# Four stacked graph-attention layers: the last stages of the last pairs turn and spread through TensorE instead of through transfers

## The chip, the core and the metric

The kernel runs on one core of one Trainium2 chip. A core has five engines with a queue of instructions each: TensorE (PE in the profile; its weight loads are PEld), VectorE (DVE), ScalarE (ACT), GpSimd (POOL) and SyncE (SP), which here only issues transfers (DMA). Each queue is worked off in its order, and engines wait for each other by semaphores. The metric is the device time in microseconds (us), a median over runs.

## The reference

Each of 128 graphs has 128 nodes with 512 features, and a 128 x 128 adjacency matrix. Four layers follow one another, each `x = layernorm(x + attention(x, adj))`. In short:

```
for layer in (L0, L1, L2, L3):            # x: (128 graphs, 128 nodes, 512 features)
    e    = leaky_relu(s_src[:, :, None] + s_dst[:, None, :], 0.2)   # per head
    attn = softmax(where(mask(adj), e, -inf))
    x    = layernorm(x + f(attn @ h(x)))
# L0: 1 head, h(x) = x
# L1: two nested layers: 4 heads of 256 (x @ W1, elu), then 1 head of 512 (h @ W2); the mask is turned
# L2: 8 heads of 64 (x @ W)
# L3: 1 head, f = elu
```

All is in 32-bit floats. An attention needs one score of every node along the rows (a column, a bias of ScalarE) and the other score along the free axis, the same in all 128 partitions (the column "spread"). Its weights come out as rows by columns and must be turned before they can be multiplied by TensorE; so must `x` before a projection.

## The kernel before

Graphs are worked on in 64 pairs (two graphs, `g`). `pair(n)` writes the work of one pair as a list of operations: `first` (layer L0), a projection by w1 in Strassen's seven products (`strassen`, the matmuls of line 711), `second` (the four-headed half of L1), a projection by w2, `third` (its one-headed half), a projection by w3, `fourth` (layers L2 and L3, and the output, line 976). Nothing is executed yet. `plan` gives each operation a due time: the length of the longest chain of work behind it, stretched by `STRETCH`; pair n starts 44.5 us (`PACE`) after pair n - 1. `lay_out` then walks through all operations with a model of costs and chooses for every engine the next operation that can start, the earliest due one first. This gives a fixed order for each queue; at run time the queues keep it, whatever the waits are. It also places the tiles in SBUF (one large `arena`) and in the eight PSUM banks. Several pairs are in work at any time; after the last pair has entered, the queues run empty, and what is left is the last pairs' later stages.

Three helpers matter here.

- `spread(cols)` brings columns of scores along the free axis. VectorE turns a broadcast of them in blocks of 32 (line 598), a transfer writes the turned rows to DRAM (line 602, tile `row`), and one or two transfers read them back into all 128 partitions (line 607, tile `db`).
- `turned(srcs, n)` turns n tiles of 128 x 128. VectorE turns the 32 x 32 blocks (line 620, into `zb`), a transfer writes them to DRAM (line 624, `scr`), and another reads them back with the blocks exchanged (line 633, or 628 for `second`; into `pt`).
- `attend(db, h0, nh, src, mask)` is the softmax of nh heads: the leaky relu on ScalarE, out of `db` into a PSUM bank (line 647); the mask and the row's extreme on VectorE (line 654, which at the same time writes its rows in the block order that `turned` expects); the exponential with its sum on ScalarE (line 663); the reciprocal (line 671); where asked for, a multiplication by it on GpSimd (line 673).

`norm` is the layer norm: statistics on VectorE (lines 682 and 686), the root on ScalarE (691, 692), the offset on GpSimd (697, 698), the scaling on ScalarE (702). `mixed` is the matmul attention times values (line 780), `resid` adds the residual on VectorE (786); `sums` prepares Strassen's left sides on GpSimd (734).

`third` calls `spread` with 2 columns, `turned` with 2 tiles, and `turned` with 8 tiles (x2, for w3). `fourth` calls `spread` with 16 columns, `turned` with 8 tiles for each graph, the matmuls of the eight heads (line 934, scaled by lines 940, and added to x2 by GpSimd on line 945), a norm, four small GpSimd operations (956 to 959) for the scores of L3, `spread` with 2 columns, `turned` with 2 tiles, `mixed`, then elu (ACT 968, DVE 970), the residual (POOL 974), a norm, and the output. So a pair issues 6 such transfers in `third` and 11 in `fourth`. In `first`, `x1` is normed in place, turned, and b2 is added to it on GpSimd into a second tile `xb` (line 846).

Of the kernel before, what the change touches and what calls it, by code (L numbers as in the profile page):

```python
# [13 lines left out]
AF = mybir.ActivationFunctionType  # L14
ALU = mybir.AluOpType
# [9 lines left out]


STRETCH, PACE, AHEAD = 1.28, 44.5, 80.0
HOP = {"PE": 0.0, "DVE": 0.0, "ACT": 0.5, "POOL": 1.0, "SP": 2.0}
SEED, SPREAD = 1, 0.0
BANKS, PRODUCTS = 8, 2  # L30
SEES = {"PE": 0.06, "DVE": 0.06, "ACT": 0.06, "POOL": 0.06, "SP": 0.0}
TAIL = {"PE": 0.165, "DVE": 0.09, "ACT": 0.1, "POOL": 0.05, "SP": 0.0}
# [69 lines left out]
def plan(ops):  # L102

    before = needs(ops)
    after = [[] for _ in ops]
    for k, need in enumerate(before):
        for q in need:
            after[q].append(k)
    left = [0.0] * len(ops)
    for k in reversed(range(len(ops))):  # L110
        left[k] = ops[k].least() + HOP[ops[k].engine] + max((left[q] for q in after[k]), default=0.0)
    rng = random.Random(SEED)
    return [STRETCH * (max(left) - left[k]) + SPREAD * rng.random() for k in range(len(ops))]


def lay_out(ops):
# [142 lines left out]
def tile_gat_stack(  # L259
# [316 lines left out]
    def bank():  # L576
        return Buf("ps", [P, 512])
# [9 lines left out]

    def spread(cols, split=1):

        n = sum(k for _, k in cols)  # L590
        sT, row = Buf(f"sT{n}", [P, n, 32]), Buf(f"row{n}", [n, P])
        a = 0
        for (b, col), k in cols:
            def turn(col=col, a=a, k=k):
                c, o = col(), sT.ap[:, a : a + k, :]
                if len(c.shape) > 2:
                    o = o.rearrange("p (a b) c -> p a b c", a=c.shape[1])
                nc.vector.transpose(o, c.unsqueeze(len(c.shape)).to_broadcast([*c.shape, 32]))

            op("DVE", 0.06 + 0.04 * k, turn, [b], joins=[sT])  # L600
            a += k
        op("SP", 0.6, lambda: nc.sync.dma_start(
            out=row.ap.rearrange("h (b c) -> b h c", b=P // 32), in_=sT.ap[0:P:32]
        ), [sT], [row], dma=0.03 + 0.01 * n, desc=4 * n)
        dbs, m = [Buf(f"db{n // split}", [P, n // split, P]) for _ in range(split)], n // split
        for i, db in enumerate(dbs):
            op("SP", 0.5, lambda i=i, db=db: nc.sync.dma_start(
                out=db.ap.rearrange("p h j -> p (h j)"),
                in_=row.ap[i * m : (i + 1) * m].rearrange("h j -> (h j)").partition_broadcast(P),
            ), [row], [db], dma=0.06 + 0.1825 * m, desc=P)  # L610
        return dbs

    def turned(srcs, n, moving=False):


        zb, scr = Buf(f"zb{n}", [P, 4, n, 32]), Buf(f"scr{n}", [P, n * P])
        o = Buf(f"pt{n}", [P, 4, n, 32] if moving else [P, n, P])
        m = n // len(srcs)
        for a, (b, src) in enumerate(srcs):
            op("DVE", 0.075 + 0.134 * m, lambda a=a, src=src: nc.vector.transpose(  # L620
                zb.ap[:, :, a * m : (a + 1) * m, :].rearrange("p b h c -> p h b c"),
                src().rearrange("p h (b c) -> p h b c", c=32),
            ), [b], joins=[zb])
        op("SP", 0.5, lambda: nc.sync.dma_start(
            out=scr.ap, in_=zb.ap.rearrange("p b h c -> p (b h c)")
        ), [zb], [scr], dma=0.05 + 0.19 * n, desc=P)
        if moving:
            op("SP", 0.58, lambda: nc.sync.dma_start(
                out=o.ap.rearrange("p q h c -> p q (h c)"),
                in_=scr.ap.rearrange("p f -> (p f)").rearrange("(q p e) -> p q e", q=4, p=P),  # L630
            ), [scr], [o], dma=0.215 * n, desc=4 * P)
        else:
            op("SP", 0.7, lambda: nc.sync.dma_start(
                out=o.ap.rearrange("p h (q c) -> p h q c", q=4),
                in_=scr.ap.rearrange("p f -> (p f)").rearrange("(q p h c) -> p h q c", q=4, p=P, h=n),
            ), [scr], [o], dma=0.415 * n, desc=4 * P * n)
        return o

    def attend(db, h0, nh, src, mask, scaled=False):

        z = bank()
        zz, nm, rs, ri = (Buf(f"{t}{nh}", s) for t, s in (
            ("zz", [P, nh, P]), ("nm", [P, nh]), ("rs", [P, nh]), ("ri", [P, nh])))

        def prelu():
            for h in range(nh):
                nc.scalar.activation(  # L647
                    z.ap[:, h * P : (h + 1) * P], db.ap[:, h0 + h, :], AF.Prelu, bias=src[1]()[:, h : h + 1], alpha=SLOPE
                )


        def masked():
            for h in range(nh):
                nc.vector.tensor_tensor_reduce(  # L654
                    out=zz.ap[:, h, :].rearrange("p (b a) -> p a b", b=4),
                    in0=z.ap[:, h * P : (h + 1) * P].rearrange("p (a b) -> p a b", b=4),
# [8 lines left out]
                    accum_out=rs.ap[:, h : h + 1],  # L665
                )

        op("ACT", [0.4] * nh, prelu, [db, src[0]], [z])
        op("DVE", [0.24] * nh, masked, [z, mask[0]], [zz, nm])
        op("ACT", [0.387] * nh, exp, [zz, nm], [zz, rs])  # L670
        op("DVE", 0.06, lambda: nc.vector.reciprocal(ri.ap, rs.ap), [rs], [ri])  # L671
# [133 lines left out]
    def first(n):  # L805
# [11 lines left out]
        for s, wv, init in ((1, w0d, 0.0), (0, w0s, b0t)):  # L817
# [4 lines left out]
                    accum_out=sc0.ap[:, s, g : g + 1],  # L822
                ), [x0], [jk], joins=[sc0], uses=[*w0b, b0b], port=True)
            if s:
                db, = spread([(part(sc0, 1), 2)])
        mask(m2, at, ALU.is_le)
        pm = bank()

# [5 lines left out]
        op("DVE", 0.335, lambda: nc.vector.tensor_mul(  # L834
            m1.ap, pm.ap[:, : 2 * P].rearrange("p (g j) -> p g j", g=2), over(noneye)
        ), [pm], [m1])
        zz, ri = attend(db, 0, 2, part(sc0, 0), (m0, lambda h: m0.ap[:, h, :]))
        pt = turned([part(zz)], 2)
        x1 = [Buf("x1", [P, F]) for _ in G]
        for g in G:  # L840
            resid(x1[g], mixed(pt, g, part(x0, g)), ri, g, part(x0, g))
        norm([part(b) for b in x1])
        xT = turned([(b, lambda b=b: wide_rows(b.ap)) for b in x1], 8)
        xb = [Buf("xb", [P, F]) for _ in G]
        for g in G:
            op("POOL", 1.24, lambda g=g: nc.gpsimd.tensor_add(xb[g].ap, x1[g].ap, b2t), [x1[g]], [xb[g]], uses=[b2b])
        return dict(xT=xT, xb=xb, m1=m1)

    def second(st, xl):

        m1 = st["m1"]
        scores = lambda g, s: part(xl[g], every, slice(2 * FH + 2 * s, 2 * FH + 2 * s + 2))
        db, = spread([(scores(g, 0), 4) for g in G])
        zz = []
        for g in G:
            def col(g=g):
                return Four(xl[g].ap)

            zz.append(attend(db, 4 * g, 4, (xl[g], col), (m1, lambda h, g=g: m1.ap[:, g, :]), scaled=True)[0])
        pt = turned([part(z) for z in zz], 8, moving=True)  # L860
        hT = [[Buf("hT", [P, 4, P]) for _ in range(2)] for _ in G]
        for g in G:
# [32 lines left out]
    def third(st, xl2):  # L895

        m1, xb = st["m1"], st["xb"]
        sc2 = small("sc2", 2)
        db, = spread([(part(xl2, every, 0, F // 2), 2)])
        op("DVE", 0.07, lambda: nc.vector.tensor_add(  # L900
            sc2.ap, xl2.ap[:, :, 1, F // 2], shift2.ap
        ), [xl2], [sc2], uses=[shift2], port=True)
        zz, ri = attend(db, 0, 2, part(sc2), (m1, lambda h: m1.ap[:, h, :]))
        pt = turned([part(zz)], 2)
        x2 = [Buf("x2", [P, F]) for _ in G]
        for g in G:
            resid(x2[g], mixed(pt, g, part(xl2, g, every, slice(0, F // 2)), True), ri, g, part(xb[g]))
        norm([part(b) for b in x2])
        st["x2"] = x2
        st["xT2"] = turned([(b, lambda b=b: wide_rows(b.ap)) for b in x2], 8)  # L910

    def fourth(n, st, xl3):

        x2 = st["x2"]
        at, m2, m3 = edges(n, xl3), Buf("m2", [P, 2, P]), Buf("m3", [P, 2, P])
        mask(m2, at, ALU.is_le)
        dbs = spread([(part(xl3[g], every, slice(SH, SH + 4)), H2) for g in G], 2)
        z3 = [Buf("z3", [P, H2, CH]) for _ in G]
        x3 = [Buf("x3", [P, F]) for _ in G]
        sc4, sz = small("sc4", 2, 2), small("sz", 2, 2)  # L920
# [1 line left out]
            op("POOL", 0.2, lambda g=g: nc.gpsimd.tensor_copy(sc4.ap[:, g, :], xl3[g].ap[:, :, C3 - 1]), [xl3[g]], joins=[sc4])  # L922
        for g in G:
            both = [attend(
                dbs[g], 4 * q, 4, part(xl3[g], q, slice(SH + 4, SH + 8)), (m2, lambda h, g=g: m2.ap[:, g, :])
            ) for q in range(2)]
            pt = turned([part(zz) for zz, _ in both], 8)
            for q in range(2):
# [30 lines left out]
            nc.gpsimd.tensor_add(sc4.ap, sc4.ap, sw.ap)  # L959

        op("POOL", 0.9, normed, [sc4, sz, rd, md], [sc4, sw], uses=[swf])
        db, = spread([(part(sc4, every, 1), 2)])
        zz, ri = attend(db, 0, 2, part(sc4, every, 0), (m3, lambda h: m3.ap[:, h, :]), scaled=True)
        pt = turned([part(zz)], 2)
        y = Buf("y", [P, 2, F])
        pas = [mixed(pt, g, part(x3[g])) for g in G]
# [10 lines left out]
            out=out[2 * n : 2 * n + 2].rearrange("g p f -> p g f"), in_=y.ap  # L977
        ), [y], [], dma=1.58, desc=2 * P)

    def pair(n):  # L980
        st = first(n)
        xT = st["xT"]
        xl = [Buf("xl1", [P, 2, N1]) for _ in G]
# [2 lines left out]
        for j in range(2):  # L986
            cols = slice(j * C1, (j + 1) * C1)
            strassen(left, s, w1s, 2, C1, cols, lambda g, h, cols=cols: xl[g].ap[:, h, cols], xl, w1_ready)
        hT = second(st, xl)
        xl2 = Buf("xl2", [P, 2, 2, C2])  # L990
        left = [[part(t) for t in both] for both in hT]
        strassen(left, sums(left, [P, 4, P]), w2s, 4, C2, slice(0, C2), lambda g, h: xl2.ap[:, g, h, :], [xl2, xl2], w2_ready)
        third(st, xl2)
        xT2 = st["xT2"]
        xl3 = [Buf("xl3", [P, 2, C3]) for _ in G]
        left = [[part(xT2, slice(4 * g + 2 * a, 4 * g + 2 * a + 2)) for a in range(2)] for g in G]
        strassen(left, sums(left, [P, 2, P]), w3s, 2, C3, slice(0, C3), lambda g, h: xl3[g].ap[:, h, :], xl3, wh_ready)
        fourth(n, st, xl3)

    pairs = B // 2  # L1000
    offsets = None
    for n in range(pairs):
        begin = len(ops)
        pair(n)
        if offsets is None:
            own = ops[begin:]
            offsets = plan(own)
        for o, t in zip(ops[begin:], offsets):
            o.due = n * PACE + t

    names = {}

# [50 lines left out]
```

## Time and profile before

| what | value |
|---|---|
| median of 3 runs (lowest, highest) | 3069.99 us (3069.07, 3072.15) |
| profiled execution: its time, its span | 3071.79 us, 3070.0 us |
| PE, DVE, ACT, POOL busy | 94 %, 84 %, 80 %, 72 % of the span |
| DMA engines, mean over the span | 605.64 MB moved, 197 GB/s |
| mean granted TensorE clock | 0.975 of full speed |
| the outputs of the last six pairs (58 to 63) are issued at | 2915.96, 2953.41, 2990.66, 3022.76, 3048.01 and 3066.22 us |

The page lists busy time by engine, the span in forty slices (a digit is a busy share in tenths), the DMA queues, the chain of work that ended last, and the costliest groups of instructions. In a timeline row stand the start, the duration, the engine, the line, the operation with output and input tiles, a count where equal ones are merged, and in brackets how long the engine had been idle and what ended that. In a row of a table by stretches stand, for each engine, busy us and the number of instructions; then the granted clock, the share of the DMA engines, and GB/s. A 32-bit matmul is two MATMUL instructions in the trace, a turning on TensorE one.

### The profile page before, as it was taken

The numbers are of one execution on the slowest core, as the hardware profiler recorded it, in microseconds if no ns is written. First come the engines' busy times: TensorE is split into PE (matmuls) and PEld (weight loads), VectorE is DVE, ScalarE is ACT, GpSimd is POOL, SyncE is SP. The second block draws the span as 40 slices with busy tenths as digits, with TensorE's granted clock in tenths as the row PEclk, the third lists the DMA queues.
The fourth block names the chain that finished last, engine by engine and source line by source line (L and its number), as shares of the span: only waits on it lengthen the run. The fifth ranks groups of instructions, "written<-read, shape, count | busy, mean of one in ns | idle before, by whom it ended". The sixth has DMA issues, their size and how long they took to land.

```text
span 3070.0 us, 56562 instructions
## 1 busy us (share of the span) xinstructions
PE 2876.5 (94%) x14054; PEld 2347.5 (76%) x14054; DVE 2585.8 (84%) x9269; ACT 2445.8 (80%) x8229; POOL 2215.9 (72%) x2859
## 2 busy tenths in 40 slices
PE   5799999999999999999999999999999999999863
PEld 3588778888888888888888888887888888888742
DVE  4768888898888889889888988898898889888763
ACT  2367888888888888888888888888888888888763
POOL 4766677777777777777777777777777777877632
PEclk8799999999999999999999999999999999999986
DMA  3369899999899999999999999989989999988774
GB/s 109 95 159 202 194 207 219 201 208 220 199 213 211 219 200 211 213 212 206 210 221 196 213 209 216 204 208 221 197 215 207 219 202 208 223 196 207 179 149 93
DMA packets 1500859, 605.64 MB, mean 197 GB/s; under 512 B 1285962, under 2 KB 1400650, under 8 KB 1500532
## 3 DMA queue, kind: packets, MB, share of 16 engines
q1 hardware_dynamic: 1499164, 598.87, 86.2%
q8 instruction: 114, 1.87, 0.3%
q14 instruction: 213, 1.74, 0.2%
q0 software_dynamic: 576, 2.10, 0.2%
q10 hardware_dynamic: 792, 1.06, 0.1%
HBM read 374.43 MB, written 227.48 MB: 196 GB/s over the span
## 4 chain that ended last, share of the span: by engine, by line
PE 44%; ACT 22%; DVE 15%; issue 4%; DMA 1%; POOL 1%; DVEq 0%; ACTq 0%; SPq 0%; POOLq 0%
PE ps L711 31%; ACT ps L647 10%; PE ps L934 6%; PE ps L780 5%; DVE arena L620 4%; DVE st L682 3%; ACT arena L702 3%; DVE arena L756 3%; ACT arena L968 2%; ACT arena L663 2%; DVE arena L654 2%; ACT arena L879 2%; ACT arena L719 2%; DVE arena L786 1%; DMA arena<-scr 1%
## 5 line engine op out<-in xcount | busy, mean ns | idle before, releaser
L734 POOL TENSOR_TENSOR arena<-arena 128x256 f32<-128x256 f32 (+1 forms) x768 | 682.1, 903 | 238.2 <-DVE arena L880 80.1
L711 PE MATMUL ps<-w1s,arena 128*128 128x258 f32 x3584 | 810.5, 383 | 36.1 <-DMA arena<-scr 35.7
L711 PEld LDWEIGHTS ps<-w1s,arena 128*128 128x128 f32 x3584 | 683.6, 191 | 192.8 <-issue 55.3
L711 PE MATMUL ps<-w2s,arena 128*128 128x257 f32 x3584 | 822.4, 380 | 4.9 <-DVE arena L880 3.0
L711 PEld LDWEIGHTS ps<-w2s,arena 128*128 128x128 f32 x3584 | 678.8, 190 | 139.1 <-issue 30.1
L663 ACT ACTIVATE arena<-arena,nm 128x128 f32<-128x128 f32 x1920 | 742.0, 396 | 30.9 <-DVE nm L654 28.9
L654 DVE CUSTOM_DVE_ANT_0 arena<-ps,arena 128x128 f32<-128x128 f32 x1920 | 531.1, 381 | 189.6 <-ACT ps L647 186.4
L647 ACT ACTIVATE ps<-arena 128x128 f32<-128x128 f32 x1536 | 564.1, 371 | 89.7 <-DMA arena<-row 52.1
L620 DVE STREAM_TRANSPOSE arena<-arena 128x512 f32<-128x512 f32 (+1 forms) x832 | 527.9, 635 | 83.0 <-ACT arena L702 52.0
L711 PE MATMUL ps<-w3s,arena 128*128 128x273 f32 x1792 | 475.9, 400 | 67.2 <-ACT arena L719 42.4
L719 ACT COPY arena<-ps 128x258 f32<-128x258 f32 (+2 forms) x1024 | 346.7, 377 | 197.9 <-PE ps L711 182.4
L711 PEld LDWEIGHTS ps<-w3s,arena 128*128 128x128 f32 x1792 | 329.6, 192 | 140.9 <-issue 50.0
L702 ACT ACTIVATE arena<-arena,mr,rd 128x512 f32<-128x512 f32 x512 | 401.3, 811 | 24.8 <-POOL mr L698 24.8
L780 PE MATMUL ps<-arena 128*128 128x512 f32 x768 | 375.0, 610 | 25.6 <-DMA arena<-scr 16.3
L663 ACT ACTIVATION_READ_ACCUMULATOR arena<-arena,nm 128x1 f32 x1920 | 373.9, 195 | 0.0
L756 DVE TENSOR_TENSOR arena<-ps,arena 128x258 f32<-128x258 f32 (+2 forms) x768 | 311.3, 412 | 68.8 <-PE ps L711 47.8
L682 DVE BATCH_NORM_STATS2 st<-arena 128x6 f32<-128x512 f32 x512 | 343.1, 680 | 13.6 <-POOL arena L945 6.9
L791 POOL TENSOR_SCALAR arena<-arena 128x256 f32<-128x256 int32 x256 | 299.0, 1168 | 32.3 <-DMA arena<-in_adj_dram 8.6
L864 POOL TENSOR_TENSOR arena<-arena,b1t 128x512 f32<-128x512 f32 x256 | 318.8, 1276 | 0.1
L673 POOL TENSOR_TENSOR arena<-arena,ri 128x512 f32<-128x512 f32 (+1 forms) x192 | 172.6, 899 | 193.7 <-DVE ri L671 189.8
L654 DVE DVE_READ_ACCUMULATOR2_ANT nm<- 128x1 f32 x1920 | 288.0, 150 | 0.0
L934 PEld LDWEIGHTS ps<-arena 128*128 128x128 f32 x2048 | 244.3, 196 | 35.6 <-issue 22.8
(85 smaller groups left out, 3516.1 us busy)
## 6 DMA issues: line engine op xcount, KB each, us to landing
scr<-arena SPq DMA_DIRECT2D x320, 512.0 KB
arena<-scr SPq DMA_DIRECT2D x320, 512.0 KB
arena<-row SPq DMA_DIRECT2D x192, 512.0 KB
arena<-in_x_dram SPq DMA_DIRECT2D x64, 512.0 KB
out_dram<-arena SPq DMA_DIRECT2D x64, 512.0 KB
arena<-row SPq DMA_DIRECT2D x192, 128.0 KB
scr<-arena SPq DMA_DIRECT2D x192, 128.0 KB
arena<-scr SPq DMA_DIRECT2D x192, 128.0 KB
```

What stands on the lines that cost most here:

```text
L620: op("DVE", 0.075 + 0.134 * m, lambda a=a, src=src: nc.vector.transpose(zb.ap[:, :, a * m : (a + 1) * m, :].rearrange("p b h c -> p h b c" ...
L647: nc.scalar.activation(z.ap[:, h * P : (h + 1) * P], db.ap[:, h0 + h, :], AF.Prelu, bias=src[1]()[:, h : h + 1], alpha=SLOPE)
L654: nc.vector.tensor_tensor_reduce(out=zz.ap[:, h, :].rearrange("p (b a) -> p a b", b=4), in0=z.ap[:, h * P : (h + 1) * P].rearrange("p (a b ...
L663: nc.scalar.activation(zz.ap[:, h, :], zz.ap[:, h, :], AF.Exp, bias=nm.ap[:, h : h + 1], scale=-1.0, accum_out=rs.ap[:, h : h + 1],)
L682: op("DVE", 0.585, lambda g=g, y=y: nc.vector.bn_stats(st.ap[:, g, :], y()), [b], joins=[st])
L702: op("ACT", 0.715, lambda g=g, y=y: nc.scalar.activation(y(), y(), AF.Identity, bias=mr.ap[:, g : g + 1], scale=rd.ap[:, g : g + 1]), [b, ...
L711: nc.tensor.matmul(px.ap[:, :w], lhsT=lhs(k), rhs=rhs(k), start=(fresh and k == 0), stop=(k == nk - 1), skip_group_check=True,)
L719: op("ACT", 0.04 + w / 1200, lambda: nc.scalar.copy(to(), px.ap[:, :w]), [px], outs, joins)
L734: op("POOL", cost, lambda: nc.gpsimd.tensor_tensor(out=own[o][1](), in0=a[1](), in1=b[1](), op=what), [a[0], b[0]], [s[o]])
L756: op("DVE", 0.05 + wide / 960, lambda: nc.vector.tensor_add(to(g, h), px.ap[:, :wide], u.ap[:, :wide]), [px, u], joins=[out[g]])
L780: op("PE", 0.885, lambda: nc.tensor.matmul(pa.ap.rearrange("p (s c) -> p s c", s=2) if paired else pa.ap, lhsT=pt.ap[:, h, :], rhs=xv[1]() ...
L934: nc.tensor.matmul(pa.ap[:, u * CH : (u + 1) * CH], lhsT=pt.ap[:, h, :], rhs=xl3[g].ap[:, q, u * CH : (u + 1) * CH], start=True, stop=True,)
```

## The change

`pair` now sets a flag, `quick`, ahead of each stage. By `QUICK = (0, 0, 0, 1, 2)` it is on in `third` of the last pair (63) and in `fourth` of the last two (62 and 63), and off everywhere else. Where it is on:

- `spread` multiplies, for each column, a broadcast of it (as the weights) by the identity, up to four columns to a PSUM bank; the leaky relu reads the bank. No line 598, 602 or 607.
- `turned` turns each tile on TensorE into a PSUM bank, four to a bank, and VectorE or ScalarE copies the bank to `pt`. For x2 (`ordered`) the columns are first put in the block order by a copy, one graph on VectorE and one on ScalarE. No line 620, 624, 628 or 633.
- `attend` masks without the block order.

Two other edits: the offsets of `plan` are computed for each kind of pair (which stages are quick), and `STRETCH` is applied later, which leaves an ordinary pair's due times as they were; and in `first` b2 is added to `x1` in place, so that this addition must follow the turning of `x1`. `FIRST` and `LAST` are empty.

```diff
+QUICK = (0, 0, 0, 1, 2)
+FIRST, LAST = (), ()
...
     def spread(cols, split=1):
         n = sum(k for _, k in cols)
+        if quick[0]:
+            rows = []
+            for (b, col), k in cols:
+                for lo in range(0, k, 4):
+                    px, m = bank(), min(4, k - lo)
+
+                    def across(col=col, lo=lo, m=m, px=px):
+                        c = col()
+                        for u in range(m):
+                            v = lo + u
+                            one = c[:, v : v + 1] if len(c.shape) == 2 else c[:, v // c.shape[2], v % c.shape[2] : v % c.shape[2] + 1]
+                            nc.tensor.matmul(
+                                px.ap[:, u * P : (u + 1) * P], lhsT=one.to_broadcast([P, P]), rhs=ident, start=True, stop=True,
+                            )
+
+                    op("PE", 0.225 * m, across, [b], [px])
+                    rows += [(px, lambda px=px, u=u: px.ap[:, u * P : (u + 1) * P]) for u in range(m)]
+            return rows
...
-    def turned(srcs, n, moving=False):
+    def turned(srcs, n, moving=False, ordered=False):
...
+        if quick[0]:
+            for a, (b, src) in enumerate(srcs):
+                if ordered:
+                    own = Buf("own", [P, m, P])
+                    def order(own=own, src=src, copy=(nc.vector.tensor_copy, nc.scalar.copy)[a % 2]):
+                        copy(own.ap.rearrange("p k (r b) -> p k r b", b=4), src().rearrange("p k (b r) -> p k r b", b=4))
+                    op(("DVE", "ACT")[a % 2], 0.06 + 0.137 * m, order, [b], [own])
+                    b, src = own, lambda own=own: own.ap
+                for lo in range(0, m, 4):
+                    px, w = bank(), min(4, m - lo)
+                    def flip(src=src, lo=lo, w=w, px=px):
+                        for u in range(w):
+                            nc.tensor.transpose(px.ap[:, u * P : (u + 1) * P], src()[:, lo + u, :], ident)
...
+                    op("PE", 0.12 * w, flip, [b], [px])
+                    op(("DVE", "ACT")[(lo // 4 + a) % 2], 0.06 + 0.137 * w, taken, [px], joins=[o])
+            return o
...
     def attend(rows, src, mask, scaled=False):
...
+                if plain:
+                    nc.vector.tensor_tensor_reduce(out=zz.ap[:, h, :], in0=z.ap[:, h * P : (h + 1) * P], in1=mask[1](h), ...)
+                    continue
...
     def first(n):
-        xb = [Buf("xb", [P, F]) for _ in G]
         for g in G:
-            op("POOL", 1.24, lambda g=g: nc.gpsimd.tensor_add(xb[g].ap, x1[g].ap, b2t), [x1[g]], [xb[g]], uses=[b2b])
-        return dict(xT=xT, xb=xb, m1=m1)
+            op("POOL", 1.24, lambda g=g: nc.gpsimd.tensor_add(x1[g].ap, x1[g].ap, b2t), [x1[g]], [x1[g]], uses=[b2b])
+        return dict(xT=xT, xb=x1, m1=m1)
...
+    quick = [False]
+
     def pair(n):
+        def stage(k):
+            quick[0] = k == 0 and n < QUICK[0] or n >= B // 2 - QUICK[1 + k]
+        stage(0)
         st = first(n)
...
+        stage(3)
         fourth(n, st, xl3)
```

## The prediction

> **What bounds the kernel now.** First the page: TensorE is busy 94% of the span at a granted clock of full speed, except in the first three and the last two slices.
>
> ```profile
> PE 2876.5 (94%) x14054; PEld 2347.5 (76%) x14054; DVE 2585.8 (84%) x9269; ACT 2445.8 (80%) x8229; POOL 2215.9 (72%) x2859
> ...
> PE   5799999999999999999999999999999999999863
> ...
> PEclk8799999999999999999999999999999999999986
> ```
>
> Then the table by stretches, for one pair in the middle and for the end.
>
> ```profile
> 1400.00:1444.67 44.67, 43.82 (x220) 36.08 (x219) 39.66 (x144) 37.95 (x129) 33.79 (x44) 1.00 0.94 210
> ...
> 2910.00:2940.00 30.00, 30.00 (x154) 25.11 (x153) 18.27 (x62) 19.49 (x58) 12.03 (x18) 0.94 0.72 171
> 2935.20:3070.00 134.80, 57.71 (x210) 39.53 (x209) 65.22 (x247) 70.58 (x233) 41.17 (x74) 0.67 0.55 114
> ```
>
> A pair in the middle takes 44.67 us, of which TensorE works 43.82: nothing but TensorE sets the pace there. From about 2935 us no engine is busy for more than 53% of the time, and the clock falls to 0.67: these 135 us are waits in a row. The chain that ended last names them (start, length, engine or transfer):
>
> ```profile
> 2993.07 6.86 DMA arena<-scr
> 2999.98 3.69 PE ps L934 x16
> 3015.02 5.18 ACT arena L663 x27
> 3025.42 6.97 DMA arena<-scr
> 3032.53 3.67 PE ps L934 x16
> 3053.15 2.70 DMA arena<-scr
> 3055.99 3.77 PE ps L780 x4
> ```
>
> `arena<-scr` is the second half of `turned`: 6.9 us for eight tiles, 2.7 for two. The timeline shows the rest of the last `spread` and `turned` of pair 63:
>
> ```profile
> 3041.21 0.55 SPq L602 DMA_DIRECT2D row<-sT  x1
> 3042.85 0.33 SPq L607 DMA_DIRECT2D arena<-row  x1
> 3047.89 0.76 ACT L647 ACTIVATE ps<-arena,sc 128x128 f32<-128x128 f32 x2
> ...
> 3050.90 0.45 DVE L620 STREAM_TRANSPOSE arena<-arena 128x256 f32<-128x256 f32 x1 [0.73 <-POOL arena L673]
> 3051.38 0.32 SPq L624 DMA_DIRECT2D scr<-arena  x1
> 3053.15 0.60 SPq L633 DMA_DIRECT2D arena<-scr  x1
> ```
>
> From turned scores to the relu 6.7 us (3041.21 to 3047.89), from weights to the matmul at 3055.99 5.1 us.
>
> **What the change touches.** The built order of every queue is the one of before up to a point near the end, where the rows of before stand at about 2935 (TensorE after pair 60's heads, ScalarE after three of pair 61's four relus). So 2935 us stay as they are, but for two edits:
>
> - The in-place addition of b2 (line 846) must now follow the turning of x1. In the trace it starts 67 to 69 us after that (pairs 8 to 63; 47 at the least): the wait is always over, 0 us; it would cost only if that slack went.
> - Pair 63's two additions move ahead on GpSimd, from 2903.88 to 2864.66, before pair 60's four sums (2866.27 to 2869.10). These end 1 us later, and TensorE takes the first at 2872.34: 0 us. At the old place 2.5 us come free, while TensorE waits there for a transfer: 0 us.
>
> Removed, one `third` and two `fourth`: 6 + 2 x 11 = 28 transfers from SP's queue, and on VectorE 4 + 2 x 8 = 20 block transposes (0.24 to 0.71 us each). What remains on SP is pair 60's and 61's; pair 61's block transfers no longer share the queue with those of 62 and 63.
>
> Added on TensorE: 38 broadcasts (2 + 2 x 18; 76 matmul instructions) and 46 turnings (10 + 2 x 18). Nearest rows: the 128x128 matmuls of line 872 follow each other at 0.112 us at full clock (each loads its weights), the turnings of line 831 at 0.108. So 76 x 0.112 + 46 x 0.108 = 13.5 us at full clock, 27 at half. Added copies: `order` twice (one each), 13 banks to `pt` (8 on VectorE, 5 on ScalarE), priced by line 968, 128x512 out of PSUM, 0.62 us in a row. The relu out of PSUM is bounded by 968 (PSUM, 0.69) and 702 (SBUF, 0.80), same shape: not dearer. I keep line 647's 0.38. The mask without block order is at most line 654's 0.23 in a row.
>
> **The sum**, along the new order, from rows of before.
>
> A, pair 63's `third`. TensorE is through pair 60's heads at 2939.1. Broadcast 0.5 and 0.2 to be seen: 2939.8, where ScalarE is through with the three relus. Two relus 0.8, pair 59's two exponentials (968) 1.5 with their matmuls, four relus 1.6, two exponentials 0.8: 2944.7. Turning, copy, two `mixed` with two residuals and statistics on VectorE, behind pair 61's transpose there: 2950.6. Meanwhile ScalarE does a root and pair 61's 16 exponentials (16 x 0.385 = 6.2), which stand ahead of pair 63's root: 2951.9. Offset 0.5, another root 0.6, two copies 0.7, two scalings 1.5, `order` 0.7: 2955.9. Eight turnings and sight 1.1, pair 59's scalings ahead of the copy 0.4, copy 0.7: **2958.1**. In before, x2's transfer has landed at 2984.06.
>
> B, TensorE's queue from there to the first broadcast of pair 62: nine w3 products at 0.87 (7 of pair 63, 2 of pair 62), five broadcasts of four columns at 0.9, pair 61's heads 3.7: 16.0 at full clock, 0.6 of waits for copies. TensorE is nearly unbroken, as in 2910:2940, so the clock of that row, 0.94: 16.6/0.94 = 17.7, **2975.8**.
>
> C, ScalarE's queue, full from here: relus of pair 62 four times 1.5, 16 exponentials of pair 63 6.2, 16 of pair 62 6.2, four copies 2.6, root 0.5, pair 60's two exponentials 1.25, 22.75: **2998.6**.
>
> D, pair 62's end. [...] half clock, as the 3.65 us of 16 head matmuls at 3032.53 show: heads 7.3, scaling 0.5, sum 1.2, statistics 1.0, root 0.6, two offsets and the four small operations 2.0, broadcast 1.2: 3012.4. Relu to weights as in before (3047.89 to 3050.90) 3.0, turning and copy 1.3: 3016.7. From `mixed` to the last residual as in before (3055.99 to 3062.53) 6.5: 3023.2. The pairs 61 to 63 now end together, and GpSimd's residuals stand in one line: an offset and pair 61's two additions, 3.0: 3026.2. From there norm and output as in before (3062.53 to 3070) 7.5: **3033.7**, 36 less than the span. The median lies as the span does (3069.99 to 3070.0), so I predict **3034 us**. Pair 61's own transfers lie beside this: its eight-tile ones have some 18 us from its exponentials (2951.9) to its heads in B, against 1.8 and 6.9 each; its last ones start when its root is through (about 2985) and take 10 to 25 us with its place in ScalarE's queue, against `mixed` at 3020.
>
> **Bounds.** Below: ScalarE still has 46 relus, 58 exponentials, 20 scalings of 0.74, 10 roots of 0.5, 8 copies of 0.3, 16 of 0.62: 71.9 us. From 2939.8 without any wait, and the 3.8 from last scaling to end: 3015.5. With the full clock everywhere B shrinks by 1 and D by about 5: 3027.5. Above: half clock throughout makes B 33: 3049.
>
> [...]
>
> **The rivals.**
>
> 1. TensorE becomes the bound. Its work after 2935.5: 14 products 12.2, 16 heads 14.7, 12 `mixed` 11.4, the new 13.5, 51.8 at full clock, 104 at half: 3039, and 12 from the last matmul's result to the end: about 3050. For: 0.67. Against: that low clock came with long gaps, which B fills.
> 2. ScalarE waits less than I sum, because three pairs side by side fill each other's gaps: 3016 to 3028, say 3024. For: ScalarE is the busiest engine there (70.58 of 134.80). Against: the end of a pair is a chain of small steps.
> 3. Slower: the weight loads of the new tiles don't lie under matmuls. There are 122; line 780's loads take 0.33 us near the end (mean over 2985:3070). In one line on TensorE at half clock: 3050 + 40 = 3090. It decides from 0.2 us a load (3050 + 0.2 x 122 = 3074). Against: 16 head matmuls of 66 columns, each with its own load, take 0.228 apiece at half clock, loads included.
> 4. The change takes away transfers that were covered: no change, 3070. Against: the chain above waits on them by name, 16.5 us in the quoted part alone.
>
> **Chances.** Forecast (3028 to 3042) 0.60; rival 1 (3042 to 3052) 0.17; rival 2 0.18; rivals 3 and 4 0.03 and 0.02. The range leaves out 3 and 4, the lower quarter of 2 and the upper end of 1: 3020 to 3050. About 0.2% (6 us) is what a measurement of this kernel can tell: faster 0.95, same 0.02, slower 0.03.
>
> **What would show it.** Right: the order of time up to 2935 unchanged; pair 63's w3 products from about 2958 instead of 2984; the last three outputs within some 6 us, the last at about 3030; no idle TensorE of 15 to 21 us waiting for `arena<-scr`; ScalarE at over 70% from 2935 on. Wrong: TensorE without gaps at 0.5 (rival 1), turnings over 0.3 us apart (rival 3), or a last output held by pair 61's `arena<-scr`.

## The result, and the profile after

The changed kernel takes 3029.77 us (median; 3027.97 to 3030.41) against 3071.07 us for the kernel before on the same chip: a ratio of 0.9865, with a 95% interval of 0.9848 to 0.9882, 41.3 us less. 3034 was forecast, 3020 to 3050 the range. The profiled execution took 3029.18 us, with a span of 3027.2 us at a mean granted clock of 0.982. The outputs of pairs 60, 63, 62 and 61 are issued at 3002.13, 3017.78, 3020.61 and 3023.14 us.

In the kernel after the lines have moved. Those used below: 605 is the broadcast on TensorE, 660 the turning and 667 its copy out of PSUM, 648 the ordering copy, 700 the leaky relu (647 before), 722 the exponential (663), 750 and 751 the root (691, 692), 756 the offset (697), 761 the scaling (702), 770 a Strassen product (711), 778 its copy (719), 839 `mixed` (780), 992 the head matmuls (934), 1003 the sum x3 (945), 1026 and 1028 the elu (968, 970), 1032 the last residual (974), 1034 the output (976).

First the page of the changed kernel, busy time, TensorE by slices, and its clock:

```profile
PE 2887.4 (95%) x14176; PEld 2357.9 (78%) x14176; DVE 2577.2 (85%) x9258; ACT 2447.5 (81%) x8235; POOL 2225.2 (74%) x2859
...
PE   5799999999999999999999999999999999999987
...
PEclk8799999999999999999999999999999999999997
```

TensorE has 122 instructions more (76 for the broadcasts, 46 turnings); its last two slices read 87 (63 before), and those of its clock 97 (86 before). Then the table by stretches of the same kernel: the whole end, and its parts.

```profile
2935.20:3027.20 92.00, 65.11 (x292) 47.35 (x290) 51.59 (x211) 67.78 (x224) 39.22 (x73) 0.75 0.32 68
2958.00:2976.00 18.00, 16.82 (x125) 14.67 (x124) 9.43 (x56) 13.45 (x55) 7.02 (x8) 1.00 0.37 51
2968.30:2989.70 21.40, 19.45 (x102) 14.83 (x100) 15.95 (x93) 20.82 (x88) 6.50 (x11) 0.74 0.04 7
2976.00:2999.00 23.00, 19.47 (x88) 16.10 (x86) 15.66 (x65) 18.87 (x69) 9.87 (x20) 0.55 0.04 7
2989.70:3027.20 37.50, 18.41 (x49) 11.14 (x49) 16.35 (x51) 21.38 (x51) 17.54 (x33) 0.59 0.18 63
```

From 2935.2 on the kernel now takes 92 us instead of 134.8 (the same work begins some 6 us sooner, see below), with ScalarE (the fourth busy time) at work for 74% of it. Three kinds of stretch follow each other: TensorE busy for 93% at full clock (2958 to 2976), ScalarE full (20.82 of 21.40 us from 2968.3 to 2989.7), and then, to the end, no engine above 57%. Rows on TensorE from the chain that ended last, of the changed kernel:

```profile
2951.76 6.72 PE ps L770 x28
2961.22 2.68 PE ps L605 x24
2963.89 3.54 PE ps L992 x32
2983.57 4.72 PE ps L660 x12
2988.29 6.74 PE ps L992 x32
3003.67 3.78 PE ps L839 x4
3008.40 3.80 PE ps L839 x4
```

Where the chain of before went through `arena<-scr` three times in the rows shown, the 75 longest pieces of this one after 2935 hold no transfer. The waits after 2935 say the same. In the kernel before, the longest one on a transfer was (us in total, times, longest)

```profile
PE ps L934 <- DMA arena<-scr: 29.4, 6, 21.3
```

and the largest of any kind in the changed kernel, where a single wait on a transfer is left (0.7 us, of GpSimd), is

```profile
POOL md L756 <- ACT rd L751: 16.6, 5, 6.5
```

**The stages.** These rows of the timeline of the changed kernel bound them: pair 60's heads, pair 63's w3 products, the first relu of pair 62, the copies that close ScalarE's stretch, and the last three outputs.

```profile
2929.73 3.68 PE L992 MATMUL ps<-arena 128*128 128x66 f32 x32
2951.76 4.42 PE L770 MATMUL ps<-w3s,arena 128*128 128x273 f32 x18 [0.84 <-DVE arena L667]
2968.46 1.47 ACT L700 ACTIVATE ps<-ps,arena 128x128 f32<-128x128 f32 x4 [2.09 <-PE ps L605]
2988.80 1.05 ACT L667 COPY arena<-ps 128x512 f32<-128x512 f32 x2
3017.78 5.73 SPq L1034 DMA_DIRECT2D out_dram<-arena  x3
```

| stage | predicted us | measured us | how measured |
|---|---|---|---|
| pair 60's heads begin at | 2935.5 | 2929.7 | first row |
| A, to pair 63's x2 turned and copied | 22.6 | 22.0 | to 2951.7, ahead of the second row |
| B, to pair 62's first relu | 17.7 | 16.8 | to 2968.5 |
| C, ScalarE's queue | 22.8 | 21.4 | to 2988.80 + 1.05 = 2989.85 |
| D, pair 62's end and the output | 35.1 | 37.3 | to the span's end, 3027.2 |

From pair 60's heads on that is 97.5 us, where 98.2 were forecast and the kernel before took 134.5: 37.0 saved there, 36.3 forecast. The other 5.8 us of the span were saved earlier, where the forecast had nothing.

**The earlier 5.8 us.** The start of a semaphore wait that opens pair 10's heads, and 35 pairs later pair 45's, in the kernel before (the first figure after the comma is the start of the first of two):

```profile
L934 PEldq EVENT_SEMAPHORE  x2: 51/51/51, 702.8 to 747.5; - x2
L934 PEldq EVENT_SEMAPHORE  x2: 51/51/51, 2265.8 to 2310.5; - x2
```

and in the changed kernel:

```profile
L992 PEldq EVENT_SEMAPHORE  x2: 51/51/51, 703.9 to 748.5; - x2
L992 PEldq EVENT_SEMAPHORE  x2: 51/51/51, 2263.4 to 2307.9; - x2
```

(2265.8 - 702.8)/35 = 44.66 us a pair before, (2263.4 - 703.9)/35 = 44.56 after. The changed kernel is 1.1 us later at pair 10 and 3.9 us sooner at pair 57 (heads at 2802.23 against 2806.14). Of the remaining 1.8 us, 1.7 are of another kind. Behind a wait of 2.43 us that both kernels have, TensorE of the kernel before multiplies more slowly:

```profile
2878.59 1.31 PE L711 MATMUL ps<-w3s,arena 128*128 128x273 f32 x4 [2.43 <-ACT arena L719]
2879.70 3.47 PE L711 MATMUL ps<-w2s,arena 128*128 128x257 f32 x8
```

than that of the changed kernel:

```profile
2874.56 1.16 PE L770 MATMUL ps<-w3s,arena 128*128 128x273 f32 x4 [2.42 <-ACT arena L778]
2875.56 1.90 PE L770 MATMUL ps<-w2s,arena 128*128 128x257 f32 x8
```

Eight matmuls take 3.47 instead of 1.90 us; over 2879.7 to 2883 the granted clock of before is 0.52, and the weight loads take 0.34 instead of 0.19 us, for 3.3 us. This is not the change's doing: behind the same wait (2.42 us each) the kernel with the addition in place alone takes 3.38 us for these eight, and a second execution of the changed kernel 2.16 us for the four ahead of them (1.16 above) and 2.58 for the eight; the kernel without the addition in place takes 1.90 again (its wait is 2.43 us).

### The profile page after: what moved, and what is told of

Read it like the earlier page. It is cut to its first block, busy times and chain, and to the rows that moved or that the text cites. A ratio compares the mean times of both kernels' runs of the same rounds, so it can differ in the third digit from the quotient of the medians.

```text
span 3027.2 us, 56473 instructions
## 1 busy us (share of the span) xinstructions
PE 2887.4 (95%) x14176; PEld 2357.9 (78%) x14176; DVE 2577.2 (85%) x9258; ACT 2447.5 (81%) x8235; POOL 2225.2 (74%) x2859
## 4 chain that ended last, share of the span: by engine, by line
PE 46%; ACT 21%; DVE 14%; issue 4%; POOL 0%; DMA 0%; ACTq 0%; DVEq 0%; POOLq 0%
PE ps L770 32%; ACT ps L700 10%; PE ps L992 7%; PE ps L839 6%; DVE arena L673 3%; DVE st L741 3%; DVE arena L815 3%; ACT arena L761 2%; ACT arena L1026 2%; ACT arena L937 2%; ACT arena L722 2%; DVE arena L713 2%; ACT arena L778 2%; DVE arena L845 1%; PE ps L930 1%
## 5 line engine op out<-in xcount | busy, mean ns | idle before, releaser
L713 DVE CUSTOM_DVE_ANT_0 arena<-ps,arena 128x128 f32<-128x128 f32 x1882 | 521.1, 382 | 176.0 <-ACT ps L700 167.6
L700 ACT ACTIVATE ps<-arena 128x128 f32<-128x128 f32 x1504 | 552.6, 371 | 86.1 <-DMA arena<-row 49.3
L673 DVE STREAM_TRANSPOSE arena<-arena 128x512 f32<-128x512 f32 (+1 forms) x819 | 518.9, 635 | 76.1 <-ACT arena L761 54.0
L761 ACT ACTIVATE arena<-arena,mr,rd 128x512 f32<-128x512 f32 x512 | 401.2, 810 | 25.1 <-POOL mr L757 25.1
```

The lines of the kernel that those rows point to most:

```text
L700: nc.scalar.activation(z.ap[:, h * P : (h + 1) * P], rows[h][1](), AF.Prelu, bias=src[1]()[:, h : h + 1], alpha=SLOPE)
L713: nc.vector.tensor_tensor_reduce(out=zz.ap[:, h, :].rearrange("p (b a) -> p a b", b=4), in0=z.ap[:, h * P : (h + 1) * P].rearrange("p (a b ...
L761: op("ACT", 0.715, lambda g=g, y=y: nc.scalar.activation(y(), y(), AF.Identity, bias=mr.ap[:, g : g + 1], scale=rd.ap[:, g : g + 1]), [b, ...
```

## The experiments

Ratios are to the kernel before on the same chip, with 95% intervals.

**The edit in place alone.** The changed kernel with the flags off: every transfer is back, and of the change only the addition of b2 to x1 in place remains. The queues' order is that of before.

```diff
-QUICK = (0, 0, 0, 1, 2)
+QUICK = (0, 0, 0, 0, 0)
```

> Only the in-place addition of b2 is kept, no stage is quick (QUICK all zero); every queue has the order of before. The changed kernel reached the end of its steady part 5.0 us earlier (44.55 us a pair against 44.67), which the prediction had at nothing. Theory I (the in-place edit, by the other places of the tiles, makes the pairs shorter): 44.55 us a pair here, about 3065 to 3066 us. Rival II (it comes with the quick stages, or differs from build to build): 44.67 us a pair, 3070 to 3071 us.

Measured: 3066.82 us, ratio 0.9987 (0.9981 to 0.9994), about 4.5 us less by the medians, 2 to 6 by the interval, where 5 to 6 were expected. From pair 10's to pair 45's heads it needs 44.57 us a pair (706.7 to 2266.5), as the changed kernel. (Its profiled execution took 3072.1 us, the longest of all 21, so only the time of a pair is read from it.)

**All but the edit in place.** The sum goes into a tile of its own again; the flags stay on.

```diff
-op("POOL", 1.24, lambda g=g: nc.gpsimd.tensor_add(x1[g].ap, x1[g].ap, b2t), [x1[g]], [x1[g]], uses=[b2b])
-return dict(xT=xT, xb=x1, m1=m1)
+op("POOL", 1.24, lambda g=g: nc.gpsimd.tensor_add(xb[g].ap, x1[g].ap, b2t), [x1[g]], [xb[g]], uses=[b2b])
+return dict(xT=xT, xb=xb, m1=m1)
```

> The changed kernel with b2 added into a tile of its own again; every queue has the order of the changed kernel. Theory I: 44.67 us a pair, about 3034 to 3035 us, which is then what the quick stages alone give, and what the prediction summed (3034). Rival II: 44.55 us a pair, 3030 us.

Measured: 3032.96 us, ratio 0.9874 (0.9859 to 0.9889), 38 us less than before and some 3 more than the changed kernel. Its pairs take 44.67 us ((2264.3 - 700.9)/35), the time of before. So the tail gives about 38 and the edit in place 3 to 4.5 by the medians, and the latter through the time of a pair. (The intervals of this run and of the changed kernel overlap, so the smaller figure rests on the time of a pair.) Among the other kernels below that add in place this time is 44.56 or 44.57 us, in a second execution of the changed kernel 44.59. With `third` alone it is 44.67, since one pair in the middle took 47.8 us (heads from 2000.99 to 2048.81); the pairs around it took 44.55.

**Is it the addition, or where the tiles lie?** With one tile fewer, the places of other tiles in SBUF move too. Here the kernel before keeps its addition and its order, and only a constant of the placing changes; of 11080 tiles of the steady part 4870 lie elsewhere.

```diff
-SLACK = 2.0
+SLACK = 1.0
```

> The kernel before, with only the places of its tiles in SBUF changed (the planner's slack between the lives of two tiles in one place, 2.0 to 1.0); 4870 of 11080 tiles of the steady part lie elsewhere, every queue has the order of before. Theory (the 0.12 us a pair that the in-place edit brought is a matter of where tiles lie): the pair time leaves 44.67 us by 0.05 or more, to either side, so the time leaves 3071 by 3 us or more. Rival (it is the addition in place itself, which needs one tile less to be written): 44.67 us a pair, within 1.5 us of 3071.

Measured: 3068.22 us, ratio 0.9995 (0.9987 to 1.0003). The same rows as above:

```profile
L934 PEldq EVENT_SEMAPHORE  x2: 51/51/51, 704.9 to 749.5; - x2
L934 PEldq EVENT_SEMAPHORE  x2: 51/51/51, 2264.5 to 2309.1; - x2
```

(2264.5 - 704.9)/35 = 44.56 us a pair, the 0.1 us without any edit of the addition. The one wait of TensorE that became shorter shows in the timeline of one pair, of before

```profile
1403.55 2.08 PE L711 MATMUL ps<-w3s,arena 128*128 128x273 f32 x8 [0.69 <-ACT arena L719]
```

and of this kernel:

```profile
1404.57 2.08 PE L711 MATMUL ps<-w3s,arena 128*128 128x273 f32 x8 [0.58 <-ACT arena L719]
```

So places alone can give the pair's 0.1 us. In the total, expected to move by 3 us or more, they are not clearly there: the medians differ by 2 us, and the interval holds no change. This execution is 2.1 us later at pair 10 already, but two executions of the changed kernel differ by 2.4 us there (703.9 and 701.5). Why a place matters stays open.

**One stage at a time.** First only `third` of pair 63, then only `fourth` of pairs 62 and 63.

```diff
-QUICK = (0, 0, 0, 1, 2)
+QUICK = (0, 0, 0, 1, 0)
```

> Quick only in the third stage of pair 63 (QUICK 0,0,0,1,0). My sum has pair 63's w3 products 26 us earlier; but the fourth stages of 62 and 63 then go through the same transfers side by side, and share ScalarE. Theory (parts don't add: each transfer that stays is on the last chain): saves 10 to 18 us, about 3052 to 3060. Rival (each part of the chain counts for itself): saves the 26 us, about 3044.

Measured: 3051.26 us, ratio 0.9936 (0.9922 to 0.9949), 20 us less; it came out just under the lower end expected. Pair 60's heads and pair 63's w3 products (36 instructions are nine products, the seven of pair 63 and two of pair 62):

```profile
2935.09 3.68 PE L992 MATMUL ps<-arena 128*128 128x66 f32 x32
2957.94 8.83 PE L770 MATMUL ps<-w3s,arena 128*128 128x273 f32 x36 [0.84 <-DVE arena L667]
```

These products start 22.9 us after pair 60's heads, nearly as soon as in the changed kernel (22.0); before it was 48.6. The outputs of the last three pairs are issued at 3029.61, 3044.37 and 3049.27.

```diff
-QUICK = (0, 0, 0, 1, 2)
+QUICK = (0, 0, 0, 0, 2)
```

> Quick only in the fourth stage of pairs 62 and 63 (QUICK 0,0,0,0,2). Pair 63's w3 products start when x2's transfer has landed, some 2984 less 5; from there w3, four broadcasts, 16 relus and exponentials and the end of a pair, 55 to 60 us. Theory: about 3038 to 3046, a saving of 25 to 32 us, most of the whole. Rival (the third stage is what counts, because all of the fourth waits for it): a saving under 18 us, over 3052.

Measured: 3044.13 us, ratio 0.9911 (0.9898 to 0.9925), 27 us less, inside what was expected; pair 63's w3 products start at 2979.65, 49.7 us after pair 60's heads, as late as before. Each of the two holds the edit in place, some 4 us. Without it they save 16 and 23 us, together 39, and both at once 37 to 38. So the savings add up, against the expectation for `third`; but not as the steps of the prediction do. Of the 26 us by which `third` brings pair 63's w3 products forward only 16 reach the end, and `fourth` gives 23 where the prediction has 10 behind that point. Why the two sums agree is not shown.

**One kind of transfer at a time.** Spreading on TensorE with turning through transfers, and the reverse. The first:

```diff
 def turned(srcs, n, moving=False, ordered=False):
-        if quick[0]:
+        if False:
 def attend(rows, src, mask, scaled=False):
-        z, nh, plain = bank(), len(rows), quick[0]
+        z, nh, plain = bank(), len(rows), False
```

> The changed kernel with the turning through transfers again (and its block order in the mask); only the spreading of scores goes through TensorE, in the same stages. Before, the last spread took 6.7 us to the relu and the 16-column one 13 (2994.4 to 3007.9). Theory: turning is the longer wait on the last chain (9 us for eight tiles, 5 for two), so spreading alone saves 10 to 20 us, 3051 to 3061 less the 4 of the in-place edit: 3047 to 3057. Rival (spreading is most of it): under 3042.

Measured: 3039.87 us, ratio 0.9906 (0.9893 to 0.992), 30 us less: the expectation that spreading gives 10 to 20 us beside the edit in place failed, and the rival's time came true (though turning alone, next, saves as much). What is left of transfers on TensorE's way, among its waits after 2935:

```profile
PE ps L839 <- DMA arena<-scr: 12.5, 3, 10.7
```

The second:

```diff
 def spread(cols, split=1):
-        if quick[0]:
+        if False:
```

> The changed kernel with the spreading through transfers again; only the turning goes through TensorE, in the same stages. Theory: saves 22 to 30 us beside the in-place edit's 4, so 3037 to 3045. With spreading alone, the two savings sum to the whole 38 or less if the parts hide each other, to more if each alone lets other waits come up in its place only once. Rival (turning alone brings little, since the relus still wait for their scores): over 3048.

Measured: 3038.96 us, ratio 0.9897 (0.9881 to 0.9912), 31 us less, as expected. Its table by stretches:

```profile
2976.00:2999.00 23.00, 20.32 (x74) 14.45 (x73) 12.60 (x64) 22.52 (x91) 4.37 (x11) 0.50 0.07 28
```

ScalarE works 22.52 of 23 us there. Without the edit in place the two halves save some 26 and 27 us, together 53 where both give 37 to 38. Unlike the stages they don't add up. With turning on TensorE the pairs are already where ScalarE is full. With spreading alone ScalarE works 18.80 of the same 23 us and waits on transfers remain, so for that half the reason stays open.

**Turning by an ordinary matmul.** The 46 turnings become 32-bit matmuls by the identity, with two instructions instead of one each.

```diff
-nc.tensor.transpose(px.ap[:, u * P : (u + 1) * P], src()[:, lo + u, :], ident)
+nc.tensor.matmul(px.ap[:, u * P : (u + 1) * P], lhsT=src()[:, lo + u, :], rhs=ident, start=True, stop=True)
```

> The changed kernel with the 46 turnings as ordinary 32-bit matmuls by the identity (92 matmul instructions for 46). The granted clock of the changed kernel is 0.5 from 2978 to 3012 us, although TensorE is busy 85% of 2976 to 2999. Theory [...]: with ordinary matmuls in their place the clock of that stretch is over 0.8, and the time is the same or up to 3 us less, though TensorE has 5 us more work at full clock. Rival (the clock is low because of the gaps between turnings, which wait for exponentials one by one, and the 66-column head matmuls): the clock stays under 0.7, and the time rises by 2 to 6 us.

Measured: 3032.79 us, ratio 0.9878 (0.9864 to 0.9891), 3 us more than the changed kernel by the medians, where the same or up to 3 less was expected; the intervals overlap. The table by stretches:

```profile
2976.00:2999.00 23.00, 18.20 (x131) 16.76 (x129) 16.56 (x75) 22.42 (x88) 7.69 (x14) 0.93 0.02 7
```

In the same 23 us TensorE is no longer busy than in the changed kernel (18.20 against 19.47 us), but the granted clock is 0.93 instead of 0.55 (0.57 in a second execution of the changed kernel). The work stands some 5 us later in this kernel; beside the same work (2981 to 3004) it is at least 0.82, an estimate from the 0.93, with the 5 us up to 2981 at 1.00 and the 5 us behind 2999 at 0.50, the highest and the lowest value in the tables of these runs. In the kernel without the edit in place, which also turns, the last head matmuls, behind the turnings, take 6.74 us in the chain, as in that of the changed kernel. In the timeline they take 6.93 us in the changed kernel

```profile
2988.08 6.93 PE L992 MATMUL ps<-arena 128*128 128x66 f32 x32
```

and here 3.84:

```profile
2992.71 3.84 PE L992 MATMUL ps<-arena 128*128 128x66 f32 x32
```

So the clock stays up far longer with ordinary matmuls in the turnings' place, as expected. The time is not better for it: ScalarE has 22.42 of the 23 us to do. Of the 3 us more, 2.5 lie ahead of pair 60's heads (2932.19 against 2929.73), where the two kernels do the same.

**The due times alone.** Flags off, transfers back, the addition in place kept, and the last pair due 20 us sooner, the one before it 10.

```diff
-QUICK = (0, 0, 0, 1, 2)
-FIRST, LAST = (), ()
+QUICK = (0, 0, 0, 0, 0)
+FIRST, LAST = (), (20.0, 10.0)
```

> The kernel before with its last two pairs' due times set earlier, pair 63's by 20 us and pair 62's by 10 us; every transfer kept. Queues keep their order up to about pair 59, then work of 62 and 63 moves ahead. Theory (the gain comes from the transfers taken out of the last chain, and the new order is only what they let in): 3062 to 3074 us, and pair 63 still ends on waits for arena<-scr of 15 us and more. Rival (an earlier start of the last pairs is what pays): 3050 or less.

Measured: 3076.98 us, ratio 1.0022 (1.0015 to 1.0029), slower than before and above what was expected, and 10 us slower than the edit in place alone, its nearest relative. Waits of TensorE after 2935:

```profile
PE ps L992 <- DMA arena<-scr: 25.8, 6, 15.2
PE ps L839 <- DMA arena<-scr: 24.2, 3, 16.4
```

The long waits stand where they stood. The outputs of pairs 58 and 59 move from 2915.96 and 2953.41 to 2928.73 and 2964.97: what went ahead held these up. This other order, with every transfer kept, gives nothing. The changed kernel's own order with the transfers kept was not run.

**Less for ScalarE, then for GpSimd at the end.** All copies of turned tiles, and the ordering ones, on VectorE:

```diff
-def order(own=own, src=src, copy=(nc.vector.tensor_copy, nc.scalar.copy)[a % 2]):
+def order(own=own, src=src, copy=nc.vector.tensor_copy):
...
-def taken(lo=a * m + lo, w=w, px=px, moving=moving, e=(lo // 4 + a) % 2):
+def taken(lo=a * m + lo, w=w, px=px, moving=moving, e=0):
```

> The kernel after with all copies of the turned tiles out of PSUM, and the ordering copies, on VectorE; ScalarE loses five copies of 0.62 us and one of 0.7. Theory (between 2968 and 2990 ScalarE's queue sets the time): the copies inside that stretch, four of them, no longer count, so 2 to 3 us less, 3026 to 3028. Rival (VectorE takes them no sooner, or the end is set by the small steps behind): 3029 to 3033.

Beside this, the last residuals of pairs 61 to 63 on VectorE, and one of two scalings of a norm in the stages without transfers:

```diff
+            if quick[0] and g:
+                op("DVE", 0.6, lambda g=g, y=y: nc.vector.tensor_scalar(
+                    out=y(), in0=y(), scalar1=rd.ap[:, g : g + 1], scalar2=mr.ap[:, g : g + 1], op0=ALU.mult, op1=ALU.add
+                ), [b, rd, mr], joins=[b])
+                continue
...
-            op("POOL", 1.235, lambda g=g: nc.gpsimd.tensor_add(y.ap[:, g, :], y.ap[:, g, :], x3[g].ap), [y, x3[g]], joins=[y])
+            op("DVE" if late else "POOL", 0.6 if late else 1.235, lambda g=g: (nc.vector if late else nc.gpsimd).tensor_add(
+                y.ap[:, g, :], y.ap[:, g, :], x3[g].ap
+            ), [y, x3[g]], joins=[y])
```

> The same copies on VectorE, and besides for the last pairs the final additions (61, 62, 63) moved from GpSimd (1.25 us each) to VectorE (0.65) and one of the two scalings of each norm of a stage without transfers moved from ScalarE (0.75) to VectorE. Theory (ScalarE's queue, then GpSimd's line of additions at the very end): 4 to 6 us less than after, 3023 to 3026. Rival (the end is one chain of small steps over all engines, in which no single engine is full): not over 2 us less, 3027 to 3031.

And the changed kernel beside them:

> The changed kernel once more, on the chip of the three other runs, as their measure: 3028 to 3032 us.

Measured: copies on VectorE 3027.47 us (3026.83 to 3029.29), ratio 0.986 (0.9847 to 0.9874); the end on VectorE too 3029.67 (3029.08 to 3030.47), ratio 0.9867 (0.9853 to 0.988); the changed kernel 3029.65 (3028.69 to 3031.92), ratio 0.9869 (0.9854 to 0.9884). The first lies where it was expected, 2 us lower, but the intervals overlap and its profiled span (3027.4 us, the longest of its four) is not shorter than those of the changed kernel (3027.2 and 3026.7): not shown to be faster. Counted from pair 60's heads (at 2932.17), its end takes 95.2 us, in the two executions of the changed kernel 97.5 and 96.6: a hint of 1 to 2 us. Its stretch on ScalarE is as full as ever, with other work in the copies' place:

```profile
2968.30:2989.70 21.40, 19.35 (x123) 15.90 (x123) 17.09 (x92) 20.72 (x89) 8.31 (x14) 0.91 0.04 8
```

The second failed its expectation of 4 to 6 us less; the time is that of its rival, a chain of small steps over all engines. The table by stretches of that kernel:

```profile
2999.00:3027.00 28.00, 10.57 (x18) 4.60 (x18) 14.77 (x34) 11.87 (x25) 3.33 (x12) 0.62 0.25 84
```

GpSimd's line is gone (3.33 us of 28 busy), and from pair 60's heads (2931.79) to the end it takes 95.3 us, no less than with the copies moved alone. No engine is busy for more than 14.77 of these 28 us; the rest are waits between engines.

## Why the prediction was right, and where it was off

- **The cause** is right. The runs with one stage, with one kind, without the edit in place, and with another order alone leave the removed transfers as the source of about 38 us. Rival 4 (covered transfers) is out: what was taken away stood in the chain.
- **"2935 us stay as they are"** is the step that failed. It held for the order, but "0 us" for the edit in place left out that places of tiles move with it; the runs put it at 3 to 4.5 us by the medians. Another 1.7 us of this profiled execution come from a stretch at half clock (0.52 in the kernel before) that it happened not to have.
- **A** (22.6 forecast, 22.0), **B** (17.7, 16.8): right in mechanism. (The terms of A up to 2944.7 add up to 2944.5.) B has the granted clock at 1.00, where the row 2910:2940 had lent 0.94; without that the queue was summed at 16.6.
- **C** (22.8, 21.4): right. ScalarE is busy for 97% of it.
- **D** (35.1, 37.3): too short by 2.2 us. The two matmuls of pair 62's `mixed` begin at 3008.4, 18.6 us into D against 18.1 forecast. Pair 62's last addition ends at 3014.97, 25.1 us in (24.6 forecast), pair 61's at 3018.61, 28.8 us in (27.6 forecast). TensorE and GpSimd of the changed kernel there:

```profile
3008.40 5.76 PE L839 MATMUL ps<-arena 128*128 128x512 f32 x8 [0.52 <-DVE arena L667]
...
3012.06 1.27 POOL L1032 TENSOR_TENSOR arena<-arena 128x512 f32<-128x512 f32 x1 [0.50 <-DVE arena L1028]
3013.71 1.26 POOL L1032 TENSOR_TENSOR arena<-arena 128x512 f32<-128x512 f32 x1 [0.38 <-DVE arena L1028]
3016.12 2.49 POOL L1032 TENSOR_TENSOR arena<-arena 128x512 f32<-128x512 f32 x2
```

 The forecast's line on GpSimd is there, pair 61's additions after pair 62's. But pair 62's two each wait for VectorE, and pair 61's two begin only at 3016.12: they stand behind pair 63's offset, which starts at 3015.68, just after its root (to 3015.61). From 3018.61 on norm and output take 8.6 us, not 7.5; pair 61's root stands behind pair 62's two scalings on ScalarE (to 3020.59).
- **The median as the span**: it lies 2.6 us above the span (3029.77 and 3027.2), where the one of before that the forecast used happened to equal it. So the forecast's 3034 is 4.2 us high, though its span, 3033.7, was 6.5 high: 5.8 from the start, 0.7 from the end's stages. In part the closeness is luck: A, B and C were 2.9 us too long and D 2.2 too short, and the median's distance from the span (2.6, less 0.3 of rounding) took off 2.3 more.
- **The upper bound** (3049 us, half clock throughout) was too high. B is full of ordinary matmuls and ran at 1.00 (2958 to 2976). In C, where turnings stand, the clock was 0.74 (2968.3 to 2989.7), but ScalarE sets the time there (20.82 of 21.40 us). Ordinary matmuls in the turnings' place raised it from 0.55 (2976 to 2999) to at least 0.82 beside the same work, by the estimate above, and saved no time. Rival 1 is out for this reason.
- **Rival 2** (ScalarE waits less, 3016 to 3028) comes nearer in number than in cause: the span, 3027.2 us, lies in its range, but ScalarE waits 24 of the last 92 us, and 16 of them in D. **Rival 3** is out: turnings follow at 1.09 us for eight at full clock, loads included; where they stand further apart (4.72 us for twelve, from 2983.57, at a clock of 0.50) they wait for exponentials.
- The signs named beforehand: last three outputs within 5.4 us (6 named), last at 3023.14 (about 3030, less the 5.8 of the start), w3 of pair 63 from 2951.8 (2958, less the 5.8 of the start), ScalarE at 74%, no long wait on `arena<-scr`.

## What to carry to other kernels

Where the last units of a pipeline end in a row of waits on transfers, a dearer way through an engine that is idle just there can pay; in the steady part, where TensorE works 43.82 of 44.67 us, it was not tried. The chain of waits names what to replace, and the sum of the queues behind it says how far it gets. Shorten both kinds of wait and the next full queue takes over (here ScalarE, then a chain of small steps), so parts measured alone need not add up: the two kinds of transfer did not. An edit that only changes which tiles exist also changes where others lie, and here that gave a tenth of a microsecond a round.

## What the runs showed of the hardware

- A change of SBUF places alone, same instructions in the same order, moved the time of a pair from 44.66 to 44.56 us (44.57 with the addition in place); the wait of one product shrank from 0.69 to 0.58 us.
- One wait of TensorE of 2.43 us was followed in the kernel before by 3.3 us at half clock (0.52, weight loads of 0.34 instead of 0.19 us), which cost 1.7 us. Of the five executions read there, the matmuls behind this wait were slow in three (eight in 3.47, 3.38 and 2.58 us) and not in two (1.90 us each). Why it is so in one execution and not in another, no run shows.
- 46 turnings done as ordinary matmuls, with twice the instructions, gave a granted clock of 0.93 from 2976 to 2999 us (by estimate at least 0.82 beside the same work), with no more busy time; it was 0.55 and 0.57 in two executions of the changed kernel with its turnings, and 0.71 with turnings and their copies on VectorE. 32 head matmuls behind them took 3.84 instead of 6.93 us.
